# Masked attention scores: mask, scale and row maximum in one custom VectorE instruction a head, and the sums of v's weight quarters moved into the second group's round

## The chip, the cores and the metric

One core of one Trainium2 chip runs the whole program. The engines of the core are TensorE (PE, the matrix engine, with its weight load shown as PEld), VectorE (DVE), ScalarE (ACT), GpSimd (POOL) and SyncE (SP), which here issues every transfer between HBM and SBUF. The metric is the device time of one execution in microseconds (us). The kernel before took 2445.91 us, the median of five runs that lie between 2444.66 and 2451.15 us.

## What is computed

Two layers over 128 graphs (`x`, 128 x 128 nodes x 512 features, fp32) with one 128 x 128 adjacency matrix `adj` for all. The first layer multiplies scores with the adjacency and divides by the row's norm; the second is attention with 8 heads of 64, where missing edges are masked out. After each layer stand a residual sum and a layer norm.

```python
def layer0(x):
    q, k, v = x @ Wq0.T, x @ Wk0.T, x @ Wv0.T
    rel = adj.T * (q @ k.T)
    rel = rel / norm(rel, axis=2)
    return layernorm(x + rel @ v)

def layer1(x):
    q, k, v = (split into 8 heads) x @ Wq1 + bq1, x @ Wk1 + bk1, x @ Wv1 + bv1
    scores = q @ k.T / sqrt(64)
    scores = scores + where(adj == 0, -1e9, 0)
    return layernorm(x + softmax(scores) @ v)
```

The change concerns the line with the mask: for each head and each row the kernel needs the masked, scaled scores and the negated row maximum (`nmax`), which the exponential takes as its bias.

## The kernel before

**Groups and rounds.** Four graphs make a group, so there are NG = 32 groups; `g` counts groups and `b` the graphs within one. The program is a pipeline over rounds r = -1, 0, ..., 31. Round r holds the projections of layer 0 for group r + 1 (kinds `m`, which is Wq0 and Wk0 multiplied into one matrix, and `v0`) and those of layer 1 for group r (`q`, `k`, `v1`). Softmax and output of group r's attention run into the following round.

**Projections.** Each projection is a fast matrix product: seven products of half-size blocks, and one of these seven split once more into seven of quarter size. `Projection.step` emits them. Products 1, 6, 7 and 4 accumulate in one PSUM bank (`pa`), and between them VectorE reads intermediate sums out: L454 after product 6, L464 after product 7. Product 5 has a bank of its own (`pb`). The quarter products (L399, `inner`) run in two banks `pc2` and `pc3`; VectorE adds their results to the output at L405 and L425, and the next quarter product writes the same part of the bank, so it waits for those adds. The weights' own sums for the quarters are made once, by `inner_weight_sums` (L151 to L154, eight additions of 128 x 128 for each kind), and are read by the L399 products as `wd_...`. In the first group (`plain`) nothing is split a second time; products 2 and 3 use banks `pd` and `pe`, with the adds L451 and L459.

**Order of the work.** Nothing is scheduled automatically: `with tc.manual_schedule()` emits instructions in the order of a hand-made calendar. `dense` holds the steps of the projections; `short` holds everything else, entered with `at(r, k, function, ...)` at slot 35 r + k. The tables ZERO, STEADY, QUICK, LAST and INNER give the slots: STEADY for groups 0 to 29, QUICK for group 30, LAST for group 31, and INNER the slots of the quarter products. Each engine works off its instructions in that order, and all transfers are in SP's queue in that order.

**Attention of a group.** `attn_scores` lets PE make the scores of 8 heads into two PSUM banks (`ps`, four heads each, L542), arranged as four stretches of 32 columns with the heads between them. Then VectorE writes `w` = scores x 1/8 + mask in one instruction a bank (L551, SCALAR_TENSOR_TENSOR of 128 x 512). `attn_max`, a calendar entry of its own, takes the negated row maxima of four heads at once (L561, TENSOR_REDUCE). `attn_exp` makes the exponential and row sum of one head in each ScalarE instruction (L568). `attn_spill` and `attn_stage` take `w` out to HBM and back in another arrangement (`wd`, `wl`), `attn_transpose` (L587) turns 32 x 32 blocks, and `attn_out` multiplies with v (L600) and turns the result (L603). In STEADY graphs 0 and 1 stand at slot 32 and graphs 2 and 3 at slot 49, so that two graphs' scores come together.

**The last group.** `last_scores` does the same in one instruction a bank (L667) and one maximum over 8 heads (L670), `last_exp` is at L677, and the weights are turned by PE (`pwT`, L684, copied out at L686) instead of through HBM.

**Masks.** `masks` makes `maskp` (128 x 128: 0 or -1e9, L125) and then copies it four times, interleaved, into `mask` (128 x 512, L127), so that L551 can read it for four heads at once. It is entered at slot 8 of round -1, and the sums of v's quarters (`inner_weight_sums` of `v0` on VectorE) at slot 9 of round -1, both ahead of the first group's `m` adds.

Of the kernel before, what the change touches and what calls it, by code (L numbers as in the profile page):

```python
# [14 lines left out]
NEG = -1e9  # L15
# [3 lines left out]
def kernel(  # L19
# [98 lines left out]
    mhalf = const.tile([P, G], F32, name="mhalf")  # L118
    nc.vector.memset(mhalf, -0.5)

    maskp = const.tile([P, N], F32, name="maskp")
    mask = const.tile([P, D], F32, name="mask")

    def masks():
        nc.vector.tensor_scalar(maskp, adj_sb, 0.0, NEG, op0=ALU.is_equal, op1=ALU.mult)  # L125
        for a in range(H // 2):
            nc.vector.tensor_copy(mask.rearrange("p (q a r) -> p q a r", q=A, a=H // 2)[:, :, a, :],  # L127
                                  maskp.rearrange("p (q r) -> p q r", q=A))

# [404 lines left out]
    def attn_scores(g, b):  # L536

        p = [ps_m.tile([P, A, H // 2, Q], F32, tag="m", name=f"ps_{g}_{b}_{s}") for s in range(2)]
        for a in range(H // 2):
            for s in range(2):  # L540
                r = slice(s * HD, (s + 1) * HD)
                nc.tensor.matmul(p[s][:, :, a, :], QT[g][r, a, b, :], KT[g][r, a, b, :], start=True, stop=True)  # L542

        if g == NG - 2 and b >= 2:
            w = two.tile([P, 2, A, H // 2, Q], F32, tag="xl", name=f"w_{g}_{b}")
        else:
            if b % 2 == 0:
                WP[g, b // 2] = one.tile([P, 2, 2, A, H // 2, Q], F32, tag="yT" if b else "v0", name=f"w_{g}_{b}")
            w = WP[g, b // 2][:, b % 2]
        for s in range(2):  # L550
            nc.vector.scalar_tensor_tensor(w[:, s].rearrange("p q a r -> p (q a r)"),  # L551
                                           p[s].rearrange("p q a r -> p (q a r)"), HD ** -0.5, mask,
                                           op0=ALU.mult, op1=ALU.add)
        nmax = small.tile([P, H], F32, tag="nmax", name=f"nmax_{g}_{b}")
        sums = small.tile([P, H], F32, tag="sums", name=f"sums_{g}_{b}")
        SOFT[g, b] = [w, nmax, sums]

    def attn_max(g, b):
        w, nmax, _ = SOFT[g, b]
        for s in range(2):  # L560
            nc.vector.tensor_reduce(nmax[:, s * (H // 2):(s + 1) * (H // 2)], w[:, s].rearrange("p q a r -> p a q r"),  # L561
                                    axis=AX.XY, op=ALU.max, negate=True)

    def attn_exp(g, b, i0):
        w, nmax, sums = SOFT[g, b]
        for i in (i0, i0 + 1):
            s, a = divmod(i, H // 2)
            nc.scalar.activation(w[:, s, :, a, :], w[:, s, :, a, :], AF.Exp, bias=nmax[:, i:i + 1],  # L568
                                 accum_out=sums[:, i:i + 1])

    def attn_spill(g, b, s):
# [85 lines left out]
    def last_scores(g, b):  # L657
        p = [ps_m.tile([P, H // 2, P], F32, tag="m", name=f"ps_{g}_{b}_{s}") for s in range(2)]
        for a in range(H // 2):
            for s in range(2):  # L660
                r = slice(s * HD, (s + 1) * HD)
                nc.tensor.matmul(p[s][:, a, :], QT[g][r, a, b, :], KT[g][r, a, b, :], start=True, stop=True)
        if b == 0:
            LT["w"] = one.tile([P, 2, H, P], F32, tag="qT", name=f"w_{g}")
        w = LT["w"][:, b] if b < 2 else two.tile([P, H, P], F32, tag="xl", name=f"w_{g}_{b}")
        for s in range(2):
            nc.vector.scalar_tensor_tensor(w[:, s * (H // 2):(s + 1) * (H // 2)], p[s], HD ** -0.5,  # L667
                                           maskp[:, None, :].to_broadcast([P, H // 2, P]), op0=ALU.mult, op1=ALU.add)
        nmax = small.tile([P, H], F32, tag="nmax", name=f"nmax_{g}_{b}")
        nc.vector.tensor_reduce(nmax, w, axis=AX.X, op=ALU.max, negate=True)  # L670
        sums = small.tile([P, H], F32, tag="sums", name=f"sums_{g}_{b}")
        SOFT[g, b] = w, nmax, sums, graph(g, b)

    def last_exp(g, b, s):
        w, nmax, sums, _ = SOFT[g, b]
        for i in range(s * (H // 2), (s + 1) * (H // 2)):
            nc.scalar.activation(w[:, i, :], w[:, i, :], AF.Exp, bias=nmax[:, i:i + 1], accum_out=sums[:, i:i + 1])  # L677

    def last_transpose(g, b, s):
        if b % 2 == 0 and s == 0:  # L680
# [45 lines left out]
    def last_store(g, b):  # L726
# [14 lines left out]
        ((10.5, 11.5, 10.5, 11.5), 13.5, (18, 19, 21, 22), 23, (24, 25), (25, 26), (26, 28), (31, 32, 33, 34)),  # L741
    )
    STEADY = (
        (32, (32.5, 34.5, 35, 35, 35), (35, 37), 41.5, (44, 49, 51.5, 56, 60, 64.5, 68, 68)),
        (32, (35.5, 38.5, 38.5, 41.5, 41.5), (41.5, 41.5), 42, (47.5, 49, 51, 52, 61.5, 65, 69, 69)),
        (49, (49.5, 49.5, 52.5, 52.5, 52.5), (55, 55), 57.5, (58, 67, 67, 70, 73, 75, 77, 77)),
        (49, (50.5, 55, 55, 55, 55), (56.5, 58), 60.5, (64.5, 67, 69, 74.5, 76, 82, 83, 85.5)),
    )
    QUICK = (
        (31.5, (32, 33.5, 34.5, 34.5, 35), (35, 38), 40.5, (41, 43.5, 43.5, 47.5, 48.5, 50.5, 50.5, 52.5)),  # L750
        (36, (37, 37, 37, 37, 37), (39.5, 40.5), 41.5, (44.5, 45.5, 47.5, 50, 52, 53, 55, 62)),
        (37, (37.5, 41, 41, 41, 41), (41, 41), 45.5, (47.5, 50, 57.5, 57.5, 57.5, 59, 59.5, 64)),
        (37, (39, 41.5, 42.5, 44, 47), (44, 47), 49.5, (51, 52, 57.5, 61, 61, 64.5, 68.5, 68.5)),
    )
    LAST = (
        (17, (17, 17.5), (22, 22), (24, 24.5), 29, 35, 37.5),
        (17.5, (18, 19.5), (24, 25), (28.5, 33.5), 40.5, 48.5, 48.5),
        (19.5, (20, 23.5), (28.5, 29), (31, 37), 41.5, 51, 51.5),
        (23, (26.5, 26.5), (30.5, 31), (33.5, 41.5), 51, 51, 52.5),
    )  # L760


    INNER = (
        (2.71, 3.72, 8.23, 9.24, 3.26, 7.27, 8.28, 9.29),
        (5.71, 8.72, 9.23, 9.74, 5.26, 7.27, 8.28, 8.79),
        (2.71, 3.22, 6.73, 8.74, 2.76, 5.27, 7.28, 8.79),
    )

    RES = 59
# [17 lines left out]
    for g in range(NG):  # L787

        for h in range(2):
            if g:  # L790
                at(g - 2, 12, load_staged, g, h)
                at(g - 1, 12 + 4 * h, load, g, h)
        last = g == NG - 1

        sc, no, ou, de, ln, sp, st, tr = ZERO[0 if g == 0 else 2 if last else 1]
        for h in range(2):
            at(g - 1, sp[h], x1_spill, g, h)
            at(g - 1, st[h], x1_stage, g, h)
        for i, (dh, h) in enumerate(halves):
            at(g - 2, ((25.5, 27, 28.5, 30) if g != 1 else (22, 23, 24, 25))[i], x_transpose, g, dh, h)  # L800
            at(g - 1, tr[i], x1_transpose, g, dh, h)
        for b in range(G):
            at(g - 1, sc[b], l0_score, g, b)
            at(g - 1, ou[b], l0_out, g, b)
            at(g - 1, ln[b // 2], l0_layernorm, g, b)
        at(g - 1, no, l0_norm, g)
        at(g - 1, de, l0_rstd, g)

        if last:
            at(g, 2, last_residual, g)  # L810
        for b in range(G):
            if last:
                sc, e, t, o, st, no, w = LAST[b]
                at(g, sc, last_scores, g, b)
                for i in range(2):
                    at(g, e[i], last_exp, g, b, i)
                    at(g, t[i], last_transpose, g, b, i)
                    at(g, o[i], last_out, g, b, i)
                at(g, st, last_stats, g, b)
                at(g, no, last_norm, g, b)  # L820
                at(g, w, last_store, g, b)
                continue
            s, ex, sp, st, pk = QUICK[b] if g == NG - 2 else STEADY[b]
            at(g, s, attn_scores, g, b)
            at(g, ex[0], attn_max, g, b)
            for i in range(4):
                at(g, ex[i + 1], attn_exp, g, b, 2 * i)
            for i in range(2):
                at(g, sp[i], attn_spill, g, b, i)
            at(g, st, attn_stage, g, b)  # L830
            pieces = attn_transpose, attn_out, attn_back, attn_rows, attn_sum, attn_stats, attn_norm, attn_write
            for k, f in zip(pk, pieces):
                at(g, k, f, g, b)
                if f is attn_rows:
                    at(g, RES if g < NG - 2 and b < 2 else k, attn_res, g, b)

    at(-1, 8, masks)
    at(-1, 41, layer1_weights, "k", "k")
    for k, name, eng in ((9, "v0", nc.vector), (17, "m", nc.vector), (28, "q", nc.gpsimd), (49.5, "k", nc.gpsimd),
                         (52, "v1", nc.gpsimd)):  # L840
        at(-1, k, inner_weight_sums, name, eng)

# [41 lines left out]
```

## Time and profile before

The profiled execution took 2445.74 us; its span, from the first to the last recorded instruction, is 2444.0 us.

| quantity | value |
|---|---|
| median of five runs | 2445.91 us |
| profiled execution, its span | 2445.74 us, 2444.0 us |
| busy: PE, DVE, ACT, POOL | 99%, 81%, 41%, 47% of the span |
| one steady round | 74.66 us |
| L551, 248 instructions | 153.2 us busy, 680 ns each |
| L561, 248 instructions | 157.3 us busy, 676 ns each |
| L568 exponentials, 992 | 384.0 us busy, 395 ns each |
| L405 on 128 x 128 from PSUM | 281 to 291 ns each |
| L127 mask copies, 4 | 3.5 us busy, 940 ns each |

"Busy" counts an instruction from its start to its end. Consecutive instructions of one engine overlap by some 0.1 us, so the distance between two starts, the step, is shorter than the length. A list of waits names the engine that waits, the tile and line of the waiting instruction, what ended the wait, and then the total in us, the number of waits and the longest. In a timeline the first column is the start and the second the length in us; neighbouring instructions of one kind are merged into one row (x4), whose length runs from the first start to the last end; in brackets stands how long the engine had been idle, and what ended that.

### The profile page before, as it was taken

How to read it: one execution, taken by the hardware profiler on the slowest of the kernel's cores; microseconds unless marked ns; L12 is line 12 of the kernel's file. 1: busy time of each engine (PE TensorE's matmuls, PEld its weight loads, DVE VectorE, ACT ScalarE, POOL GpSimd, SP SyncE). 2: the span in 40 equal slices, each digit the busy share in tenths (PEclk: the TensorE clock that was granted, in tenths of full speed). 3: DMA queues.
4: the chain of work that ended last, by engine and by line, in shares of the span. 5: the costliest groups of instructions: out<-in, count | busy, mean ns of one | idle time of the engine just before them, and what ended most of it. 6: DMA issues, size and time to landing. Idle time of an engine off the chain costs nothing.

```text
span 2444.0 us, 48441 instructions
## 1 busy us (share of the span) xinstructions
PE 2419.0 (99%) x16552; PEld 2130.7 (87%) x16552; DVE 1976.6 (81%) x4409; ACT 1011.9 (41%) x3211; POOL 1138.6 (47%) x1796
## 2 busy tenths in 40 slices
PE   8999999999999999999999999999999999999997
PEld 5888888888888888888888888888888888888886
DVE  6678888788888788887888887888878888878888
ACT  1244344443443443444434434434444344344354
POOL 3625534445434355344454343553444543435544
PEclk9999999999999999999999999999999999999999
DMA  7356656566565666565665656665656656566564
GB/s 161 104 129 172 171 169 170 167 174 172 168 177 157 171 173 171 167 171 166 174 172 169 177 157 170 174 170 169 175 161 174 169 169 179 158 171 173 154 176 130
DMA packets 508600, 405.17 MB, mean 166 GB/s; under 512 B 37568, under 2 KB 424768, under 8 KB 508352
## 3 DMA queue, kind: packets, MB, share of 16 engines
q1 hardware_dynamic: 508352, 402.08, 59.6%
q8 instruction: 129, 2.11, 0.4%
q14 instruction: 119, 0.97, 0.1%
HBM read 237.31 MB, written 164.63 MB: 164 GB/s over the span
## 4 chain that ended last, share of the span: by engine, by line
PE 96%; DVE 2%; DMA 1%; issue 0%; POOL 0%; SPq 0%; POOLq 0%; ACT 0%; DVEq 0%
PE pa_v L358 18%; PE pa_q L358 9%; PE pa_k L358 9%; PE pa_m L358 9%; PE pc_v L399 8%; PE ps L542 5%; PE po L600 5%; PE pst L477 5%; PE pb_v L358 5%; PE po L522 4%; PE pc_k L399 4%; PE pc_q L399 4%; PE pc_m L399 4%; PE pb_q L358 2%; PE pb_k L358 2%; PE pb_m L358 2%
## 5 line engine op out<-in xcount | busy, mean ns | idle before, releaser
L568 ACT ACTIVATE w<-w,nmax 128x128 f32<-128x128 f32 x992 | 384.0, 395 | 116.2 <-DVE nmax L561 116.1
L502 POOL TENSOR_SCALAR ve<-st 128x1 f32<-128x1 f32 (+1 forms) x160 | 45.9, 287 | 745.4 <-DVE st L498 735.3
L358 PE MATMUL pa_v<-wc_v,tx 128*128 128x256 f32 x1536 | 363.7, 380 | 0.0
L358 PEld LDWEIGHTS pa_v<-wc_v,tx 128*128 128x128 f32 x1536 | 277.4, 190 | 30.3
L517 ACT ACTIVATE xr<-xr,sh,rstd 128x512 f32<-128x512 f32 x58 | 47.2, 815 | 411.4 <-POOL sh L512 411.4
L568 ACT ACTIVATION_READ_ACCUMULATOR w<-w,nmax 128x1 f32 x992 | 191.8, 193 | 0.0
L358 PE MATMUL pa_m<-tx,wc_m 128*128 128x256 f32 x768 | 184.0, 382 | 3.1 <-DVE yT L454 2.0
L405 DVE TENSOR_TENSOR v<-pc_v,v 128x256 f32<-128x256 f32 (+1 forms) x444 | 135.2, 310 | 58.3 <-PE pc_v L399 46.5
L358 PEld LDWEIGHTS pa_q<-tx,wc_q 128*128 128x128 f32 x768 | 143.2, 190 | 44.4 <-issue 29.3
L358 PE MATMUL pa_k<-tx,wc_k 128*128 128x256 f32 x768 | 181.8, 380 | 0.0
L358 PE MATMUL pa_q<-tx,wc_q 128*128 128x256 f32 x768 | 181.6, 379 | 0.2 <-DVE qT L454 0.2
L551 DVE SCALAR_TENSOR_TENSOR w<-ps,mask 128x512 f32<-128x512 f32 x248 | 153.2, 680 | 7.3 <-PE ps L542 7.3
L561 DVE TENSOR_REDUCE nmax<-w 128x4 f32<-128x512 f32 x248 | 157.3, 676 | 0.0
L358 PEld LDWEIGHTS pa_m<-tx,wc_m 128*128 128x128 f32 x768 | 138.5, 190 | 19.1 <-DVE yT L454 2.4
L587 DVE STREAM_TRANSPOSE wT<-wl 128x1024 f32<-128x1024 f32 x124 | 154.1, 1242 | 0.3 <-DMA xl_x<-in_x_dram 0.3
L358 PEld LDWEIGHTS pa_k<-tx,wc_k 128*128 128x128 f32 x768 | 138.4, 190 | 14.9
L631 POOL TENSOR_TENSOR xr<-xr,bv_b 128x512 f32<-128x512 f32 x58 | 73.7, 1270 | 139.2 <-DMA xr<-x1d 53.4
L369 ACT ACTIVATE qT<-pa_q,bq_sb 128x256 f32<-128x256 f32 x128 | 53.6, 470 | 205.0 <-PE pa_q L358 200.3
L399 PE MATMUL pc_v<-wd_v,ux 128*128 128x128 f32 x756 | 135.8, 275 | 0.2 <-DVE v L405 0.2
L405 DVE TENSOR_TENSOR qT<-pc_q,qT 128x128 f32<-128x128 f32 (+1 forms) x320 | 96.5, 309 | 44.4 <-PE pc_q L399 36.7
L522 PE MATMUL po<-v,rel 128*128 128x512 f32 x256 | 130.5, 593 | 0.0
L542 PE MATMUL ps<-kT,qT 64*128 64x128 f32 x1984 | 129.5, 279 | 0.0
(228 smaller groups left out, 6172.5 us busy)
## 6 DMA issues: line engine op xcount, KB each, us to landing
wd<-w SPq DMA_DIRECT2D x248, 256.0 KB, 3.0
wl<-wd SPq DMA_DIRECT2D x496, 128.0 KB, 3.0
xl_x<-in_x_dram SPq DMA_DIRECT2D x256, 128.0 KB, 6.0
x<-in_x_dram SPq DMA_DIRECT2D x64, 512.0 KB, 4.5
x1d<-x SPq DMA_DIRECT2D x64, 512.0 KB, 3.1
xl_h<-x1d SPq DMA_DIRECT2D x256, 128.0 KB, 2.9
od<-oT SPq DMA_DIRECT2D x496, 64.0 KB, 2.1
o<-od SPq DMA_DIRECT2D x118, 256.0 KB, 2.9
```

The costliest lines, as they stand in the source:

```text
L358: nc.tensor.matmul(bank[:, m, :], l[:, k, m * P:(m + 1) * P], r[:, k, :], start=start and m == 0 and k == 0, stop=(m == 1 and k == 1), ski ...
L399: nc.tensor.matmul(self.c[o][:, slot, :], l, r, start=start, stop=True, skip_group_check=True)
L405: nc.vector.tensor_tensor(y, self.c[o][:, slot], s if kept else y, op=ALU.add)
L477: nc.tensor.matmul(p, XT[g][:, dc, b, :], YT[g][:, dc, b, :], start=(dc == 0), stop=(dc == C - 1))
L522: nc.tensor.matmul(p, REL[g][0][:, b, :], V0[g][:, b, :], start=True, stop=True)
L542: nc.tensor.matmul(p[s][:, :, a, :], QT[g][r, a, b, :], KT[g][r, a, b, :], start=True, stop=True)
L551: nc.vector.scalar_tensor_tensor(w[:, s].rearrange("p q a r -> p (q a r)"), p[s].rearrange("p q a r -> p (q a r)"), HD ** -0.5, mask, op0= ...
L561: nc.vector.tensor_reduce(nmax[:, s * (H // 2):(s + 1) * (H // 2)], w[:, s].rearrange("p q a r -> p a q r"), axis=AX.XY, op=ALU.max, negat ...
L568: nc.scalar.activation(w[:, s, :, a, :], w[:, s, :, a, :], AF.Exp, bias=nmax[:, i:i + 1], accum_out=sums[:, i:i + 1])
L587: nc.vector.transpose(wT, SOFT[g, b][0].rearrange("p a i r -> p i a r"))
L600: nc.tensor.matmul(p[s * HD:(s + 1) * HD, a, :], V1[g][:, b, h * HD:(h + 1) * HD], wT[:, s * (H // 2) + a].rearrange("p q t -> p (q t)"), ...
L631: nc.gpsimd.tensor_tensor(xr, xr, bv_b, op=ALU.add)
```

## The change

Instead of `maskp` and `mask` there is one `mask` of 128 x 128 with 0 or -8e9. A new function `masked` makes one instruction for one head: out = (scores + mask) x (-1/8), and the minimum of `out` over the row goes into one column of `nmax`. That minimum of the negated values is the negated maximum. `attn_scores` and `last_scores` call it eight times a graph; `attn_max` and its calendar entries are gone; the exponentials read the negated `w` and so get `scale=-1.0`. In the built program each call is two VectorE instructions, one over 128 x 128 elements and one that writes the accumulated minimum to 128 x 1. The sums of v's quarters move from slot 9 to slot 38.5 of round -1, which is slot 3.5 of round 0. A number of calendar slots change. The order of PE's matmuls stays the same up to the last two groups, where a few pieces change places; in the rounds VectorE's order differs by the masked scores and by the place of two of the four `wl` transposes among their neighbours; GpSimd's order is unchanged.

```diff
-    maskp = const.tile([P, N], F32, name="maskp")
-    mask = const.tile([P, D], F32, name="mask")
+    mask = const.tile([P, N], F32, name="mask")

     def masks():
-        nc.vector.tensor_scalar(maskp, adj_sb, 0.0, NEG, op0=ALU.is_equal, op1=ALU.mult)
-        for a in range(H // 2):
-            nc.vector.tensor_copy(mask.rearrange("p (q a r) -> p q a r", q=A, a=H // 2)[:, :, a, :],
-                                  maskp.rearrange("p (q r) -> p q r", q=A))
+        nc.vector.tensor_scalar(mask, adj_sb, 0.0, NEG * HD ** 0.5, op0=ALU.is_equal, op1=ALU.mult)
+
+    def masked(dst, scores, m, least):
+        nc.vector.tensor_tensor_reduce(out=dst, in0=scores, in1=m, scale=-HD ** -0.5, scalar=3.0e38,
+                                       op0=ALU.add, op1=ALU.min, accum_out=least)
...
-        for s in range(2):
-            nc.vector.scalar_tensor_tensor(w[:, s].rearrange("p q a r -> p (q a r)"),
-                                           p[s].rearrange("p q a r -> p (q a r)"), HD ** -0.5, mask,
-                                           op0=ALU.mult, op1=ALU.add)
         nmax = small.tile([P, H], F32, tag="nmax", name=f"nmax_{g}_{b}")
+        for i in range(H):
+            s, a = divmod(i, H // 2)
+            masked(w[:, s, :, a, :], p[s][:, :, a, :], mask.rearrange("p (q r) -> p q r", q=A), nmax[:, i:i + 1])
...
-    def attn_max(g, b):
-        w, nmax, _ = SOFT[g, b]
-        for s in range(2):
-            nc.vector.tensor_reduce(nmax[:, s * (H // 2):(s + 1) * (H // 2)], w[:, s].rearrange("p q a r -> p a q r"),
-                                    axis=AX.XY, op=ALU.max, negate=True)
...
-            nc.scalar.activation(w[:, s, :, a, :], w[:, s, :, a, :], AF.Exp, bias=nmax[:, i:i + 1],
+            nc.scalar.activation(w[:, s, :, a, :], w[:, s, :, a, :], AF.Exp, bias=nmax[:, i:i + 1], scale=-1.0,
                                  accum_out=sums[:, i:i + 1])
...
-        for s in range(2):
-            nc.vector.scalar_tensor_tensor(w[:, s * (H // 2):(s + 1) * (H // 2)], p[s], HD ** -0.5,
-                                           maskp[:, None, :].to_broadcast([P, H // 2, P]), op0=ALU.mult, op1=ALU.add)
         nmax = small.tile([P, H], F32, tag="nmax", name=f"nmax_{g}_{b}")
-        nc.vector.tensor_reduce(nmax, w, axis=AX.X, op=ALU.max, negate=True)
+        for i in range(H):
+            s, a = divmod(i, H // 2)
+            masked(w[:, i], p[s][:, a], mask, nmax[:, i:i + 1])
...
     STEADY = (
-        (32, (32.5, 34.5, 35, 35, 35), (35, 37), 41.5, (44, 49, 51.5, 56, 60, 64.5, 68, 68)),
-        (32, (35.5, 38.5, 38.5, 41.5, 41.5), (41.5, 41.5), 42, (47.5, 49, 51, 52, 61.5, 65, 69, 69)),
-        (49, (49.5, 49.5, 52.5, 52.5, 52.5), (55, 55), 57.5, (58, 67, 67, 70, 73, 75, 77, 77)),
-        (49, (50.5, 55, 55, 55, 55), (56.5, 58), 60.5, (64.5, 67, 69, 74.5, 76, 82, 83, 85.5)),
+        (32, (32.5, 34.5, 35, 35, 35), (35, 36.5), 41.5, (44, 49, 51.5, 56, 60, 64.5, 68, 68)),
+        (32, (35.5, 38.5, 38.5, 41.5, 41.5), (41.5, 41.5), 42, (47.5, 49, 51, 52, 60, 65, 69, 69)),
+        (49, (49.5, 49.5, 50.5, 50.5, 52.5), (55, 55), 57.5, (58.5, 67, 67, 70, 73, 75, 77, 77)),
+        (49, (50.5, 55, 55, 55, 55), (56.5, 56.5), 60.5, (63.5, 67, 69, 74.5, 76, 82, 83, 85.5)),
     )
...
     LAST = (
-        (17, (17, 17.5), (22, 22), (24, 24.5), 29, 35, 37.5),
-        (17.5, (18, 19.5), (24, 25), (28.5, 33.5), 40.5, 48.5, 48.5),
-        (19.5, (20, 23.5), (28.5, 29), (31, 37), 41.5, 51, 51.5),
-        (23, (26.5, 26.5), (30.5, 31), (33.5, 41.5), 51, 51, 52.5),
+        (17, (17, 17.5), (20, 22), (24, 24.5), 29, 35, 37.5),
+        (17.5, (17.5, 19.5), (24, 24.5), (28, 31), 40, 45.5, 46),
+        (19.5, (20, 23.5), (28.5, 29), (31, 37), 41, 51, 51),
+        (23, (23.5, 27), (29.5, 32), (33.5, 41.5), 51, 53, 54.5),
     )
...
     INNER = (
         (2.71, 3.72, 8.23, 9.24, 3.26, 7.27, 8.28, 9.29),
-        (5.71, 8.72, 9.23, 9.74, 5.26, 7.27, 8.28, 8.79),
-        (2.71, 3.22, 6.73, 8.74, 2.76, 5.27, 7.28, 8.79),
+        (5.71, 8.72, 9.23, 9.74, 4.26, 7.27, 8.28, 8.79),
+        (2.71, 3.22, 6.73, 8.24, 2.76, 4.77, 6.78, 8.79),
     )
...
-            at(g, ex[0], attn_max, g, b)
...
-    for k, name, eng in ((9, "v0", nc.vector), (17, "m", nc.vector), (28, "q", nc.gpsimd), (49.5, "k", nc.gpsimd),
+    for k, name, eng in ((38.5, "v0", nc.vector), (17, "m", nc.vector), (28, "q", nc.gpsimd), (49.5, "k", nc.gpsimd),
                          (52, "v1", nc.gpsimd)):
```

## The prediction

> **What bounds the kernel now.** I read the page's first part, then TensorE's (PE's) waits, then the timelines of PE and VectorE (DVE) at the start, in one steady round and at the end.
>
> ```profile
> PE 2419.0 (99%) x16552; PEld 2130.7 (87%) x16552; DVE 1976.6 (81%) x4409; ACT 1011.9 (41%) x3211; POOL 1138.6 (47%) x1796
> ```
>
> ```profile
> PE pa_m L358 <- DVE yT L454: 2.0, 1, 2.0
> ```
>
> PE is busy 99% of the span and its named waits come to some 15 us, each met once or twice. A steady round (from one `po` L600 at 1199.25 to the next at 1273.91 us: 74.66 us) has no PE wait at all. So work taken off DVE in the rounds is worth nothing. The change can win only at the start and the end, and can lose wherever DVE now answers PE late.
>
> **The change, part by part.**
>
> *1. The start.* Four mask copies go, and the eight sums of v's quarters leave.
>
> ```profile
> 33.99 3.52 DVE L127 COPY mask<-maskp 128x128 f32<-128x128 f32 x4
> ...
> 43.95 0.68 DVE L454 TENSOR_TENSOR yT<-pa_m,yT 128x512 f32<-128x512 f32 x1
> ```
>
> ```profile
> 40.77 1.89 PE L358 MATMUL pe_m<-xT,wc_m 128*128 128x256 f32 x8
> 44.69 1.99 PE L358 MATMUL pa_m<-tx,wc_m 128*128 128x256 f32 x8 [2.04 <-DVE yT L454]
> ```
>
> The columns are start, length, engine, line. The add L454 stands behind copies (3.52) and sums (L151 to L154, twice, 37.43 to 43.95: 6.5 us). Its own input, the product at 37.31, ends at 39.20. In the changed order only the one mask instruction (0.94 at 33.01) stands ahead, so L454 starts at 39.2 and PE goes on at 40.77 + 1.73 = 42.50 instead of 44.69: 2.19 us, and the 0.10 by which the first matmul after a wait is longer (1.99 against 1.89 for eight). I take -2.3. The later waits there (L464, ACT yT, POOL sq) are chains of their own and move along; the DMA share is 0.00 in 50 to 60 us, so no load is late for the next group.
>
> The sums come back in the next round, behind the first two adds of `pc_m`, at 67.85 on before's clock. Eight equal sums (wd_m, 47.40 to 49.59) took 2.2 us. Cover: PE needs the pair of adds behind them at 72.95, and 67.85 + 2.2 + 0.6 = 70.65. Without it (GpSimd busy beside them, as in 37.43 to 43.95) they take 6.5, the pair ends at 74.95, and 2.0 us of the gain is given back. I take 0: GpSimd runs mostly short instructions there until 70.13.
>
> *2. The masked scores in the rounds.* For each sequence two L551 and two L561 become eight instructions, and in the built program each is two: the 128-element pass and a read of its accumulator into one column of `nmax`. Step from start to start decides, not length.
>
> ```profile
> 1202.41 2.49 DVE L551 SCALAR_TENSOR_TENSOR w<-ps,mask 128x512 f32<-128x512 f32 x4 [0.22 <-PE ps L542]
> ...
> 1205.67 0.62 DVE L405 TENSOR_TENSOR v<-pc_v,v 128x128 f32<-128x128 f32 x2 [0.77 <-PE pc_v L399]
> 1206.20 1.27 DVE L561 TENSOR_REDUCE nmax<-w 128x4 f32<-128x512 f32 x2
> ```
>
> ```profile
> 1207.20 0.61 PE L399 MATMUL pc_v<-wd_v,ux 128*128 128x128 f32 x4
> ```
>
> An L551 steps by (2.49 - 0.68)/3 = 0.60, an L561 by 0.60, so a sequence costs DVE 2.4 us. The new pass reads 128 elements from PSUM and a mask from SBUF, as L405 does, which steps by 0.21 where nothing holds it:
>
> ```profile
> 1245.72 0.29 DVE L405 TENSOR_TENSOR v<-pc_v,v 128x128 f32<-128x128 f32 x1
> 1245.93 0.41 DVE L405 TENSOR_TENSOR v<-pc_v,s_v 128x256 f32<-128x256 f32 x1
> ```
>
> The accumulator read on DVE is in no row. Bounds:
>
> ```profile
> 0.80 0.09 DVE L117 MEMSET ones<- 128x32 f32 x1 [0.80 <-PEq L870]
> 0.83 0.06 DVE L119 MEMSET mhalf<- 128x4 f32 x1
> ...
> 1258.79 0.18 DVE L498 BATCH_NORM_AGGREGATE st<-bs 128x2 f32<-128x6 f32 x1
> 1258.88 0.73 DVE L629 TENSOR_TENSOR o<-o,rs 128x512 f32<-128x512 f32 x1
> ```
>
> ```profile
> 1207.28 0.19 ACT L568 ACTIVATION_READ_ACCUMULATOR w<-w,nmax 128x1 f32 x1
> 1207.37 0.39 ACT L568 ACTIVATE w<-w,nmax 128x128 f32<-128x128 f32 x1
> ```
>
> Below: a memset, which like the read has no input in memory, steps by 0.03. Above: DVE's aggregate and ScalarE's own accumulator read step by 0.09; farther out, the latter's whole length, 0.19. A head then costs p = 0.24, 0.30 or 0.40 us. I take 0.05 for the read, nearer to the memset as the row of the same engine without an input, so p = 0.26 and 8p = 2.1 us a sequence. DVE's total hardly moves; what moves is the place. Scores, mask and maximum now stand in one block, where the maxima used to stand behind the adds.
>
> The tightest place is two sequences at once. The block starts at 1202.41 and takes 16p instead of 2.4. Behind it stand the two L405 (0.61 for the pair, the second waits for the first), and in the built program the third of the four matmuls at 1207.20, at 1207.42, waits for the second L405; PE starts 0.05 after such an end (44.64 to 44.69). So 1202.41 + 16p + 0.66 <= 1207.42, p <= 0.272. At 0.26 there is 0.2 us to spare and the cost is 0. Above, each of 30 rounds loses 16(p - 0.272) + 0.11, and nothing takes it up, since PE has no other wait. The other block (1241.72, before the matmuls at 1247.38) allows 1241.72 + 16p + 0.74 + 0.05 <= 1247.38, p <= 0.304.
>
> PSUM: the first bank is freed after 4p instead of one L551; the next user, `pb_q` at 1205.47, waits for the fourth head, 1202.41 + 4p = 1203.5. ScalarE's exponentials get their first maximum some 4 us sooner and nothing else on its queue changes length. The transfers are the same in number; half-spills stand somewhat earlier on SP's queue, behind exponentials that are also earlier. The moved transposes of `wl` feed products with no PE wait now.
>
> *3. The last but one group.* Block of one sequence at 2368.56; L425 behind it is awaited by PE at 2370.58. 2368.56 + 2.08 + 0.29 + 0.05 = 2370.98: 0.40 + 0.11 lost. The following 16 heads start at about 2372.7 (scores, shifted by that), end at 2376.9, and the next L425 ends at 2377.2 against PE's 2375.71 + 0.5: 1.0 + 0.1 lost. The wait at 2379.57 (0.19 and 0.11) goes, as a maximum no longer stands there. Sum +1.3.
>
> *4. The last group.* DVE is the chain from 2405.8 on.
>
> ```profile
> 2406.52 1.29 DVE L667 SCALAR_TENSOR_TENSOR w<-ps,maskp 128x512 f32<-128x512 f32 x2
> 2407.84 1.22 DVE L670 TENSOR_REDUCE nmax<-w 128x8 f32<-128x1024 f32 x1
> 2408.98 0.68 DVE L454 TENSOR_TENSOR v<-pa_v,v 128x512 f32<-128x512 f32 x1
> ```
>
> 2.46 us a sequence become 2.08: four times 0.38, -1.5. The reordered transposes and products I take at 0, bounds -2 and +1 (a copy of 0.6 now stands ahead of L464, which PE awaits).
>
> **Sum:** -2.3 - 1.5 + 1.3 = -2.5 us on a span of 2444.0; the profiled execution took 2445.74 (1.74 around its span), 0.17 under the median of 2445.91. So 2443.4.
>
> **Rivals.**
>
> *A. DVE answers late in every round (slower).* With p = 0.30 the place at 1207.42 loses 16 x 0.028 + 0.11 = 0.56, 30 times: +16.8, or 2460 with the rest. For it: the steps of 0.09 in two rows, and that no other PE wait absorbs it. Against: the memset row. It passes 0.2% (4.9 us, about what a measurement here can tell from no change) once 30(16(p - 0.272) + 0.11) > 7.4, from p = 0.280. Chance 0.33, 0.04 of it still within 0.2%.
>
> [...]
>
> *B. The read costs ScalarE's full 0.19.* p = 0.40: 30 x (2.05 + 0.11) and, at 1247.38, 30 x (1.54 + 0.11), together +114: 2560. DVE's aggregate is as long (0.18) and steps by 0.09, so 0.08.
>
> *C. Faster.* p = 0.24 gives the last group 4 x 0.54 = 2.2 and the last but one only +0.7; the first exponential, which waits 4.77 us for `nmax` at 2409.09, comes up to 2 us sooner and with it transposes and products: -2.3 - 2.2 + 0.7 - 1.7 = -5.5, 2440.4. Against: DVE, not ScalarE, is the chain there. 0.17.
>
> *D. The sums meet GpSimd:* 2.0 of the gain is lost, 2445.4; it lies inside the forecast's own case.
>
> **How the numbers follow.** Forecast (no stall in the rounds, within 0.2%) 0.42, A 0.33, B 0.08, C 0.17. Faster 0.17, same 0.42 + 0.04 = 0.46, slower 0.29 + 0.08 = 0.37. The range goes from a little below C, 2439.5, to A at p = 0.30, 2461; about 0.18 is left out, nearly all above. The forecast's own range is 2441 to 2446.
>
> **What would show it.** The step between two heads' passes is p: below 0.272 PE has no wait on DVE at `pc_v` L399 in the rounds; above it, one wait a round on `v` L405, of 16(p - 0.272). The wait of `pa_m` on L454 at the start is gone and the eight wd_v sums take about 2.2 us. A round that is still 74.66 us long bears the forecast out; one of 75.2 is rival A.

## The result and the profile after

The changed kernel took 2442.16 us (median of 25 executions, 2441.09 to 2444.67). The kernel before took 2447.74 us (median of 43, 2444.66 to 2451.86; the first five of these gave the 2445.91 that the prediction was made against). The ratio is 0.9978, 95% interval [0.9973, 0.9984]: 0.22% faster, hardly over what a measurement here can tell from no change. The profiled execution of the changed kernel took 2444.12 us, its span is 2442.3 us.

The page's first part, busy time of each engine, and four of PE's waits in the changed kernel:

```profile
PE 2420.9 (99%) x16552; PEld 2131.6 (87%) x16552; DVE 1866.4 (76%) x5945; ACT 1005.4 (41%) x3211; POOL 1139.5 (47%) x1796
```

```profile
PE pc_v L399 <- DVE v L425: 1.3, 1, 1.3
...
PE po L695 <- DVE wT L680: 0.9, 1, 0.9
...
PE pa_m L358 <- DVE yT L464: 0.9, 1, 0.9
PE pc_m L399 <- DVE yT L405: 0.6, 1, 0.6
```

VectorE's busy time fell by 110 us, PE's rose by 1.9, and the time moved by no more than 0.2%. All waits of PE are again met once. The wait of 2.0 us on L454 is gone; one of 0.6 on L405, at 73.04, is new (before had one of 0.3 at 66.56).

Three stretches, cut at instructions that every version has, show where time goes. *Start*: from the first product of v (`pa_v`, 21.70 us before) to the product behind the first group of quarter products (`pa_m`, 73.39). *Rounds*: from there to the last group's first scores (2405.32). *End*: from there to the end of the span.

| trace | start | rounds | end | half clock seen in the start |
|---|---|---|---|---|
| before | 51.69 | 2331.93 | 38.68 | no |
| changed | 51.69 | 2332.02 | 36.92 | yes |
| changed, heads longer (below) | 49.53 | 2331.62 | 36.94 | no |

(In the other traces the rounds take 2331.8 to 2332.0.) So the rounds are worth nothing, the end gave 1.76 us, and the start gave 2.16 us in one execution and nothing in another. PE's timeline in the start of the changed kernel:

```profile
42.46 1.89 PE L358 MATMUL pa_m<-tx,wc_m 128*128 128x256 f32 x8
...
53.67 2.96 PE L358 MATMUL pa_m<-xT,wc_m 128*128 128x256 f32 x8 [1.11 <-DVE xT L212]
56.42 2.65 PE L522 MATMUL po<-v,rel 128*128 128x512 f32 x4
...
73.04 0.49 PE L399 MATMUL pc_m<-ux,wd_m 128*128 128x128 f32 x2 [0.59 <-DVE yT L405]
73.36 1.89 PE L358 MATMUL pa_m<-tx,wc_m 128*128 128x256 f32 x8
```

The product at 42.46 stood at 44.69 before: 2.23 us gained. Then two groups of matmuls take 2.96 and 2.65 us that took 1.99 and 1.88 in the kernel before: 1.74 us lost. The two rows before:

```profile
56.00 1.99 PE L358 MATMUL pa_m<-xT,wc_m 128*128 128x256 f32 x8 [1.11 <-DVE xT L212]
57.83 1.88 PE L522 MATMUL po<-v,rel 128*128 128x512 f32 x4
```

The table of one-microsecond stretches says why; after the stretch and its length come PE, PEld, DVE, ACT and POOL busy, and then the granted TensorE clock:

```profile
51.00:52.00 1.00, 0.27 (x3) 0.08 (x1) 0.29 (x1) 0.00 (x0) 0.51 (x2) 1.00 0.00 0
52.00:53.00 1.00, 0.42 (x8) 0.16 (x8) 0.38 (x2) 0.00 (x0) 0.08 (x1) 1.00 0.00 0
53.00:54.00 1.00, 0.33 (x2) 0.31 (x3) 1.00 (x2) 0.00 (x0) 0.98 (x1) 1.00 0.00 0
54.00:55.00 1.00, 1.00 (x5) 0.86 (x4) 0.96 (x3) 0.00 (x0) 0.05 (x1) 0.78 0.02 8
55.00:56.00 1.00, 1.00 (x4) 0.72 (x4) 1.00 (x2) 0.00 (x0) 0.33 (x1) 0.50 0.00 0
56.00:57.00 1.00, 1.00 (x3) 0.66 (x2) 0.97 (x2) 0.29 (x1) 0.92 (x3) 0.50 0.00 0
57.00:58.00 1.00, 1.00 (x2) 0.33 (x1) 0.20 (x1) 0.30 (x1) 1.00 (x3) 0.52 0.00 0
```

PE was busy for only 1.0 of the 3 us from 51 to 54 (it waits for the norm's chain through DVE and GpSimd), and then ran at half clock for (0.22 + 0.50 + 0.50 + 0.48) / 0.5 = 3.4 us. Its longest idle time in this place was 1.11 us. The kernel before has the same idle place at 53.5 to 56.0 (PE busy for 1.03 of the 3 us from 53 to 56) and kept full clock in its profile: 1.00 in every microsecond from 50 to 61. Why half clock follows the place in one execution and not in another, no run here shows.

The rest of the gain went to the sums of v, which met GpSimd. (Two of the seven half-size products, 2 and 3, are split into quarters and not one, as the section on the kernel before has it; hence eight sums, four for each.) VectorE's and GpSimd's timelines there:

```profile
67.84 0.29 DVE L154 TENSOR_TENSOR wc_v<-wc_v,wd_v 128x128 f32<-128x128 f32 x1
68.05 0.70 DVE L151 TENSOR_TENSOR wd_v<-wc_v 128x128 f32<-128x128 f32 x1
...
70.01 1.33 DVE L154 TENSOR_TENSOR wc_v<-wc_v,wd_v 128x128 f32<-128x128 f32 x1
71.26 0.60 DVE L405 TENSOR_TENSOR yT<-pc_m,yT 128x128 f32<-128x128 f32 x2
```

```profile
67.92 0.68 POOL L201 COPY wc_k<-wk_s 128x512 f32<-128x512 f32 x1
...
69.91 1.27 POOL L157 TENSOR_TENSOR wc_k<-wk_s,wc_k 128x512 f32<-128x512 f32 x1
```

From the moment GpSimd copies the `k` weights, a sum takes 0.6 to 1.3 us instead of 0.28. Each of the four slow sums ends 0.14 to 0.16 us behind the GpSimd instruction that was running when it started (70.01 + 1.33 = 71.34 against 69.91 + 1.27 = 71.18), as though it waited for that one. The eight take 4.3 us (66.99 to 71.26), the pair of adds behind them is late, and PE waits 0.59 us at 73.04.

The heads, in the round that the prediction worked with:

```profile
1202.04 0.29 DVE L127 CUSTOM_DVE_ANT_0 w<-ps,mask 128x128 f32<-128x128 f32 x1 [0.27 <-PE ps L542]
1202.26 0.08 DVE L127 DVE_READ_ACCUMULATOR2_ANT nmax<- 128x1 f32 x1
1202.26 0.28 DVE L127 CUSTOM_DVE_ANT_0 w<-ps,mask 128x128 f32<-128x128 f32 x1
...
1205.42 0.08 DVE L127 DVE_READ_ACCUMULATOR2_ANT nmax<- 128x1 f32 x1
1205.42 0.61 DVE L405 TENSOR_TENSOR v<-pc_v,v 128x128 f32<-128x128 f32 x2
```

```profile
1206.79 0.61 PE L399 MATMUL pc_v<-wd_v,ux 128*128 128x128 f32 x4
```

Sixteen heads take 3.38 us, so a head steps by p = 0.211 us. The accumulator read is 0.08 us long and adds nothing: the next pass starts in the same instant. The pair of adds ends at 1206.03, a microsecond before PE's third matmul (1207.01) needs it.

### The profile page after: what moved, and what is told of

It is laid out like the page before. It is cut to its first block, busy times and chain, and to the rows that moved or that the text cites. A ratio compares the mean times of both kernels' runs of the same rounds, so it can differ in the third digit from the quotient of the medians.

```text
span 2442.3 us, 49798 instructions
## 1 busy us (share of the span) xinstructions
PE 2420.9 (99%) x16552; PEld 2131.6 (87%) x16552; DVE 1866.4 (76%) x5945; ACT 1005.4 (41%) x3211; POOL 1139.5 (47%) x1796
## 4 chain that ended last, share of the span: by engine, by line
PE 96%; DVE 2%; issue 1%; DMA 1%; POOL 0%; ACT 0%; SPq 0%; POOLq 0%; DVEq 0%
PE pa_v L358 18%; PE pa_m L358 9%; PE pa_q L358 9%; PE pa_k L358 9%; PE pc_v L399 8%; PE ps L542 5%; PE po L594 5%; PE pst L477 5%; PE pb_v L358 4%; PE po L522 4%; PE pc_k L399 4%; PE pc_q L399 4%; PE pc_m L399 4%; PE pb_m L358 2%; PE pb_q L358 2%; PE pb_k L358 2%
## 5 line engine op out<-in xcount | busy, mean ns | idle before, releaser
L502 POOL TENSOR_SCALAR ve<-st 128x1 f32<-128x1 f32 (+1 forms) x160 | 56.5, 353 | 745.1 <-DVE st L498 735.7
L127 DVE CUSTOM_DVE_ANT_0 w<-ps,mask 128x128 f32<-128x128 f32 x1024 | 221.7, 286 | 16.6 <-PE ps L542 15.8
L562 ACT ACTIVATION_READ_ACCUMULATOR w<-w,nmax 128x1 f32 x992 | 198.8, 200 | 0.0
L405 DVE TENSOR_TENSOR v<-pc_v,v 128x256 f32<-128x256 f32 (+1 forms) x444 | 135.2, 309 | 69.9 <-PE pc_v L399 58.0
L405 DVE TENSOR_TENSOR qT<-pc_q,qT 128x128 f32<-128x128 f32 (+1 forms) x320 | 98.4, 315 | 54.1 <-PE pc_q L399 46.4
L366 ACT COPY yT<-pa_m 128x512 f32<-128x512 f32 x64 | 37.5, 585 | 243.4 <-DVE v L405 115.9
L627 POOL TENSOR_TENSOR xr<-xr,o 128x512 f32<-128x512 f32 x58 | 74.0, 1275 | 124.8 <-issue 122.5
```

What stands on the lines that cost most here:

```text
L127: nc.vector.tensor_tensor_reduce(out=dst, in0=scores, in1=m, scale=-HD ** -0.5, scalar=3.0e38, op0=ALU.add, op1=ALU.min, accum_out=least)
L405: nc.vector.tensor_tensor(y, self.c[o][:, slot], s if kept else y, op=ALU.add)
L627: nc.gpsimd.tensor_tensor(xr_, xr_, o.rearrange("p (f a r) -> p f a r", f=A, a=H // 2), op=ALU.add)
```

## The experiments

Theory: (1) VectorE's place in the rounds is free up to p = 0.269 and costs PE from there (the prediction's condition on the rows above: 1202.04 + 16p + 0.66 <= 1207.01); (2) the end is won by the fused instruction, the start by the shorter masks; (3) what the start wins is sometimes taken back by half clock, which in the changed kernel's profile came behind the idle place of PE (54.6 to 58.0 us), and by GpSimd. The main rivals are named in each expectation. Times are medians of the executions; "before" is the kernel before on the same chip in the same session.

**Both kernels again** (no edit).

> The kernel before, once more, for the clock and span of each execution. Theory T (half clock): the executions of before above 2449 us differ from those near 2445.5 by 3.4 us windows at half TensorE clock around the stalls of the start (42 to 56 us); each such window costs PE about 1.7 us, so an execution 4 to 5 us above the fastest should show a mean granted clock lower by some 0.002 to 0.004. Rival (loads): the clock is the same, 0.999, in all, and the time goes to transfers. Median expected 2446 to 2449.

Measured: 2447.19 us (11 executions, 2445.99 to 2451.99), before beside it 2448.39 (33), ratio 0.9999 [0.9990, 1.0008]. Over all executions of the kernel before in this study that list a clock (102): mean granted clock 0.999, 16 executions, median 2446.15 us; 0.998, 27, 2447.07; 0.997, 28, 2448.89; 0.996 or less, 31, 2451.22. Time and clock go together, as the theory said, and the rival of the transfers, with the same clock in all, falls. An execution 5 us longer shows 0.003 less clock, that is 0.003 x 2448 = 7 us of full clock; a part of it may lie behind waits, and the clock is listed only to 0.001, which is 2.4 us. Where in the kernel the clock is lost, these means do not say.

> The changed kernel, once more, to get a profile without the half clock at 54.5 to 58.0 us that its first profile shows. Theory T: median 2442.1; an execution near 2441.8 has full clock until 2430 us, its PE stands 2.2 us ahead of before from 42.5 until about 70, and keeps 1.2 to 2.0 of it behind 75 us; the end (2405 on) gives 1.7 to 2.0. Rival (the gain of the start is given back in any case by the sums of v, which meet GpSimd): PE is level with before at 75 us although no clock was lost, and the whole gain comes from the end.

Measured: 2442.71 us (11, 2441.08 to 2447.07), ratio 0.9981 [0.9972, 0.9990]. Its profile (2445.14 us) caught half clock in another place, at 24.8 to 28.2 us, behind a wait of 3.33 us for the first `x` at the very start; its start stretch is 51.09, end 36.98. That half clock cost it 1.7 us (two groups of matmuls need 2.34 and 2.87 us from start to start instead of 1.80 and 1.73), so its start would be 49.4 without. A trace without half clock anywhere in the start came from a later kernel whose start is the same (heads_longer, below), with 49.53. In both the gain is kept: the rival that it is lost in any case falls.

**The sums left where they were.**

```diff
-    for k, name, eng in ((38.5, "v0", nc.vector), ...
+    for k, name, eng in ((9, "v0", nc.vector), ...
```

> The change with the sums of v's quarters left at slot 9 of round -1. By the rows: sums start at 34.0 behind the one mask instruction, take 6.5 us beside GpSimd and end at 40.5; L454 starts there, 1.2 us later than in the changed kernel, ends at 41.2, and PE needs it only at 42.46, so PE waits for nothing there. If so the moved sums bring nothing: same time as the changed kernel or 0.3 to 0.6 us faster, 2441.6, as no sums meet GpSimd at 68 us and the wait of 0.59 us at 73.04 is gone. Rival (the sums had to move): a wait of pa_m on yT L454 of 1 us or more comes back, time 2443 or more.

Measured: 2442.52 us (11, 2441.33 to 2446.07), ratio 0.9977 [0.9968, 0.9985]; no wait on L454. Its VectorE and PE rows:

```profile
39.67 1.24 DVE L154 TENSOR_TENSOR wc_v<-wc_v,wd_v 128x128 f32<-128x128 f32 x1
40.84 0.68 DVE L454 TENSOR_TENSOR yT<-pa_m,yT 128x512 f32<-128x512 f32 x1
```

The sums take 7.3 us beside GpSimd, so L454 starts late (its input was there at 38.8), and still PE has the result before it needs it at 42.06. Both this trace and the changed kernel's first one have the half clock in the start; the start stretch is 50.82 here and 51.69 there. The moved sums thus cost 0.87 us in such an execution and bring nothing; between the medians (2442.52 and 2442.71) there is no difference, where 0.3 to 0.6 was thought possible: what made L454 late before was the sums *and* the copies, and taking away the copies is enough.

**Only the sums moved**, in the kernel before.

```diff
-    for k, name, eng in ((9, "v0", nc.vector), ...
+    for k, name, eng in ((38.5, "v0", nc.vector), ...
```

> The kernel before, with nothing but the sums of v's quarters moved to slot 38.5 of round -1. The four mask copies end at 37.5, before L454's input at 39.2, so the wait of 2.0 us at 44.69 goes here too. Theory: same start as the changed kernel, and the end of the kernel before: slower than the changed kernel by what the end gave, 1.7 to 2.0 us, so median 2443.9 and lowest 2443. If the masks and not the sums made L454 late, the wait stays and the time is before's.

Measured: 2445.89 us (11, 2443.84 to 2449.40), ratio 0.9990 [0.9981, 0.9999]. The wait on L454 is gone, the start is 52.11 with half clock, the end 38.68 as before. So either half of the edit at the start mends it. The median is 2 us over the expected 2443.9. The lowest times put the end's share at 2443.84 - 2441.08 = 2.8 us, the traces at 1.76; the 1 us between is not explained.

**A longer head**, twice.

```diff
+    fill = const.tile([P, 96], F32, name="fill")
...
             masked(w[:, s, :, a, :], p[s][:, :, a, :], ..., nmax[:, i:i + 1])
+            if g < NG - 2:
+                nc.vector.memset(fill, 0.0)
```

> The changed kernel with one more VectorE instruction behind every head in groups 0 to 29, a memset of 128 x 96 to a tile that nobody reads. It makes the step p of a head longer; the prediction's formula says what a longer p costs. A memset is expected to add 0.05 to 0.12, so p = 0.26 to 0.33. Theory (the place at 1207.42 decides, PE needs the second L405): below p = 0.269 nothing; above it each of 30 rounds loses 16 (p - 0.269) + 0.11, and above 0.304 the second block loses as well. p = 0.31 gives 30 x 0.77 + 30 x 0.2 = 29 us at most, 2465 to 2471; p = 0.29 gives 13 us, 2455. Rival (a later head costs nothing, since the adds could stand later or PE has other slack): 2442 whatever p is.

Measured: 2443.79 us (7, 2441.46 to 2444.33), ratio 0.9974 [0.9964, 0.9985], no wait of PE in the rounds. VectorE's timeline:

```profile
1200.64 0.23 DVE L128 CUSTOM_DVE_ANT_0 w<-ps,mask 128x128 f32<-128x128 f32 x1
1200.79 0.08 DVE L128 DVE_READ_ACCUMULATOR2_ANT nmax<- 128x1 f32 x1
1200.85 0.14 DVE L557 MEMSET fill<- 128x96 f32 x1
1200.90 0.23 DVE L128 CUSTOM_DVE_ANT_0 w<-ps,mask 128x128 f32<-128x128 f32 x1
```

A head now steps by 0.26, which is the p of the prediction, and it is free, as the prediction said: the trace's rounds take 2331.62 us. The median doesn't show it, being 1.1 to 1.6 us over the changed kernel's: five of the seven executions lie near 2444, where the changed kernel has 8 of 25, and so few can't tell the two apart. This profile also is the changed kernel's start without half clock (the memsets begin later). PE there:

```profile
22.11 1.97 PE L359 MATMUL pa_v<-wc_v,xT 128*128 128x256 f32 x8 [1.68 <-DVE xT L213]
...
54.21 1.99 PE L359 MATMUL pa_m<-xT,wc_m 128*128 128x256 f32 x8 [1.11 <-DVE xT L213]
56.05 1.88 PE L523 MATMUL po<-v,rel 128*128 128x512 f32 x4
...
71.64 1.89 PE L359 MATMUL pa_m<-tx,wc_m 128*128 128x256 f32 x8
```

The start is 71.64 - 22.11 = 49.53 against 51.69: 2.16 us kept. The eight sums took 66.12 to 68.49, 2.4 us: at full clock they are through when GpSimd's copies begin (68.57; in the second trace of the changed kernel 71.31 and 71.39).

The second time the memset has 128 x 144 (`fill` of [P, 144]).

> As heads_longer, where 128 x 96 made the step of a head 0.260 us and cost nothing (no wait of PE in the rounds), but the memset is 128 x 144, so p should be about 0.31. Theory (first block: p up to 0.269; second block: up to 0.304): each of 30 rounds loses 16 (0.31 - 0.269) + 0.11 = 0.77 and 16 (0.31 - 0.304) + 0.11 = 0.2 us, 29 us in all: 2471, with waits of pc_v or pc_q L399 on adds of VectorE in every round. If p comes out as 0.29: 13 us, 2455. Rival (PE has slack behind the block that the formula misses): under 2446.

Measured: 2471.53 us (4, 2469.82 to 2473.55), ratio 1.0091 [1.0077, 1.0105]; p = 0.310. PE's waits, and the wait in its timeline:

```profile
PE pc_v L400 <- DVE v L406: 15.2, 30, 0.5
```

```profile
1221.74 0.49 PE L400 MATMUL pc_v<-wd_v,ux 128*128 128x128 f32 x2 [0.51 <-DVE v L406]
```

Laid against the trace with p = 0.26, PE falls behind in each round by 0.77 us at the first block and by 0.20 at the second; 0.77 and 0.2 were expected. The rival that PE has slack there falls.

**The old instructions in the last group**, in the new calendar.

```diff
-        for i in range(H):
-            s, a = divmod(i, H // 2)
-            masked(w[:, i], p[s][:, a], mask, nmax[:, i:i + 1])
+        for s in range(2):
+            nc.vector.scalar_tensor_tensor(w[:, s * (H // 2):(s + 1) * (H // 2)], p[s], HD ** -0.5,
+                                           mask[:, None, :].to_broadcast([P, H // 2, P]), op0=ALU.mult, op1=ALU.add)
+        nc.vector.tensor_reduce(nmax, w, axis=AX.X, op=ALU.max, negate=True)
```

(The exponentials of that group lose their `scale=-1.0` again.)

> The changed kernel, but the last group's scores with the two old instructions a bank and one maximum over 8 heads (2.46 us a sequence instead of 8 x 0.211 = 1.69), in the new calendar. Theory (VectorE is the chain from 2410 on, two to four sequences of 0.77 us lie on it): 1.5 to 3.1 us slower than the changed kernel, median 2444.2 to 2445.5. Rival (the end is gained by the calendar alone): same as the changed kernel.

Measured: 2446.25 us (11, 2443.66 to 2450.58), ratio 0.9990 [0.9981, 0.9999]. PE's timeline in the end, of the kernel before, of this kernel and of the changed one:

```profile
2417.25 0.71 PE L399 MATMUL pc_v<-wc_v,ux 128*128 128x128 f32 x4 [1.88 <-DVE v L425]
```

```profile
2417.20 0.71 PE L399 MATMUL pc_v<-wc_v,ux 128*128 128x128 f32 x4 [2.92 <-DVE v L425]
```

```profile
2416.27 0.71 PE L399 MATMUL pc_v<-wc_v,ux 128*128 128x128 f32 x4 [1.34 <-DVE v L425]
```

The end is 38.82 us long, against 36.92 and 38.68 (before): the instruction is worth 1.9 us, the calendar's changes nothing (0.1 to the bad). The median lies farther off, 3.5 to 4 us, than the trace, and above the expected 2444.2 to 2445.5; whether the longer idle place of PE (2.92 us) has to do with that was not shown.

**The old instructions in groups 0 to 29**, maxima as entries of their own.

```diff
+            at(g, (32.5, 35.5, 49.5, 50.5)[b], attn_max, g, b)
```

(with L551 and `attn_max` of the kernel before, `scale=1.0` in their exponentials, and the wide mask)

> The changed kernel, but groups 0 to 29 with the old instructions and the maxima as an entry of their own at the old slots (the wide mask is copied by ScalarE in round 0). Theory (work taken off VectorE in the rounds is worth nothing): the same time as the changed kernel, median 2442.2 to 2443, round of 74.66 us, no wait of PE in the rounds. Rival (the rounds gained by the fused instruction): slower by some 30 x 0.05 = 1.5 us or more.

Measured: 2443.65 us (11, 2442.69 to 2447.91), ratio 0.9979 [0.9971, 0.9988]. That is some 1 to 1.5 us over the changed kernel, more than expected, but not in the rounds: start 51.69, rounds 2331.95, the same to 0.1 us, and PE stays level to 2421 us. The end is 37.99, 1.05 too long, and the excess lies behind all arithmetic, in SyncE's wait for the last store:

```profile
SPq L892 <- DMA out_dram<-o: 2.8, 1, 2.8
```

In the other traces this wait is 1.7 us. In this trace alone a transfer of instructions (queue q14) falls into the last 3 us of the span. That it delays the store was not tested. For the question asked the rounds are decided: the 85 us of VectorE time that the fused instruction saves there (1951.6 busy here, 1866.4 in the changed kernel) are worth nothing.

**Matmuls in PE's idle places.** The identity is multiplied with itself into banks that are overwritten.

```diff
+        if g == 0:
+            for _ in range(7):
+                nc.tensor.matmul(pn, ident, ident.rearrange("p (g q) -> p g q", g=G), start=True, stop=True)
...
+                if self.name == "m_1":
+                    for _ in range(9):
+                        nc.tensor.matmul(self.a[:, 0, 0:P], ident, ident, start=True, stop=True)
```

> The changed kernel with the sums at slot 9, and matmuls of the identity on itself (7 ahead of the first pn, 9 ahead of the first product of m of group 1; their results are overwritten) in the two places where PE stands idle at 51 to 54 us. [...] Rival (the half clock has nothing to do with PE's idle time there): the same spread, 2441.3 to 2446, median 2442.5.

Measured: 2443.32 us (8, 2442.72 to 2443.89), ratio 0.9977 [0.9967, 0.9988]. No half clock in the start, and all executions within 1.2 us; but the matmuls took 1.73 and 2.27 us in gaps of 0.86 and 1.1, so the start is 50.74 and the median lies above the 2441.5 or less that was hoped for.

> As keep_warm, where 7 and 9 matmuls took 1.73 and 2.27 us in idle places of 0.86 and 1.1 us and so cost 1.3 us themselves, but kept the half clock away in all 8 executions (2442.7 to 2443.9). Now 3 and 4 of them, 0.74 and 0.98 us, which fit. Theory T: no half clock at 50 to 60 us, median 2441.3 to 2442, nearly all executions under 2443. Rival: they are too few, spread as in the changed kernel.

Measured: 2442.18 us (7, 2441.68 to 2445.47), ratio 0.9973 [0.9962, 0.9984]: five executions under 2442.6, two near 2445. The profile is of one of these two: full clock from 50 to 60 us, but half clock at 24 to 27 us, behind a wait of 3.0 us for the first `x`, which these matmuls do not cover. In the times nothing is shown: 2 of 7 executions lie above 2443, and 8 of 25 of the changed kernel. In the profiles the place tells more: half clock follows it in seven of the eleven without such matmuls, and in none of the three with them (before_warm, next, is the third).

> The kernel before with such matmuls in its idle places at the start: 8 behind the first pe_m (42.6 to 44.6 us, ahead of the product that waits for L454), 3 ahead of pn and 4 ahead of the first product of m of group 1. No wait and no stall is removed. Theory T (what spreads the executions of before from 2445 to 2452 is the half clock after idle windows at 42 to 56 us): executions at 2445 to 2446.5, median near 2445.8, that is 2 to 3 us below before of the same chip. Rival (the spread has another cause, or comes from the end): median as before, 2447.5 to 2448.5.

Measured: 2446.53 us (11, 2444.75 to 2448.10), before beside it 2449.29 (17, 2445.88 to 2452.32), ratio 0.9989 [0.9980, 0.9998]. So its median is 2.8 us lower (0.5 to 4.9 by the interval), and the median of the mean granted clocks is 0.998 against 0.997. This is what clock lost behind idle PE at the start would give back. It is less than the theory said: six of the 11 executions lie above 2446.5. Its profile shows one more such place, in the end; PE's timeline, and rows of one microsecond, in which the third number from the end is the granted clock:

```profile
2416.85 0.71 PE L399 MATMUL pc_v<-wc_v,ux 128*128 128x128 f32 x4 [1.88 <-DVE v L425]
...
2418.70 3.52 PE L358 MATMUL pa_v<-wc_v,tx 128*128 128x256 f32 x8
```

```profile
2419.00:2420.00 1.00, 1.00 (x3) 0.82 (x3) 1.00 (x3) 0.00 (x0) 1.00 (x1) 0.50 0.00 0
2420.00:2421.00 1.00, 1.00 (x4) 0.73 (x4) 0.97 (x2) 0.00 (x0) 0.19 (x1) 0.50 0.00 0
```

This lengthens its end from 38.68 to 39.57.

**A copy of the end on ScalarE**, with the sums at slot 9.

```diff
-        copy = nc.scalar.copy if b == G - 1 and s else nc.vector.tensor_copy
+        copy = nc.scalar.copy if (b, s) in ((0, 0), (G - 1, 1)) else nc.vector.tensor_copy
```

> The changed kernel with the sums at slot 9, and the first copy of turned weights in the last group (L680, graph 0, heads 0 to 3) made by ScalarE, which stands idle from 2416.5 to 2420 us, instead of VectorE, where it takes 0.6 us ahead of L464 and L425, for which PE waits 1.34 us. Theory (that copy lies on the chain of the end): the wait of pc_v on v L425 falls to 0.7 us, the end comes 0.4 to 0.6 us sooner, lowest time 2440.6 to 2440.9 against 2441.1 to 2441.3, median about 2441.7. Rival (the chain goes through ScalarE or the scores after it): same time as the changed kernel with the sums at slot 9, 2442.5, lowest 2441.3.

Measured: 2441.56 us (10, 2440.93 to 2445.59), ratio 0.9974 [0.9964, 0.9983].

```profile
2417.70 0.71 PE L399 MATMUL pc_v<-wc_v,ux 128*128 128x128 f32 x4 [0.74 <-DVE v L425]
```

The wait fell from 1.34 to 0.74 and the end from 36.92 to 36.39, as expected. Half of the executions are at 2440.93 to 2441.20, under nearly all of the changed kernel; between medians the 0.6 us can't be told from nothing. It is the version that I would keep.

## Why the prediction came out as it did

The forecast was 2443.4 us; 2442.16 was measured, inside the range (2439.5 to 2461) and inside the forecast's own (2441 to 2446). The gain of 0.22% is on the border between the cases "within 0.2%" and "faster". That the time came so near is in part luck: the forecast started from 2445.91, which over more executions became 2447.74, and so the gain between the medians is 5.6 us and not 2.5.

*Step 1, the start, -2.3:* right in size and mechanism. PE's product was put at 42.50 and came at 42.46; of the 2.23 us, 2.16 stand behind the first quarter products when the clock holds. What the step lacked is the clock: in the first profile 1.74 us went to half clock. The sums were put at 2.2 us without GpSimd (2.4 measured) and at 6.5 beside it, with 2.0 given back (rival D); beside it they took 4.3 and gave back 0.87. In the traces they met GpSimd's copies where half clock had come just before, and not in the two where it had not.

*Step 2, the rounds:* the condition p <= 0.272 is right to a few hundredths of a microsecond (p = 0.26 free, p = 0.31 costs 0.77 + 0.20 a round), and with it the weight of rival A. The term that was mis-sized is the accumulator read: 0.05 was taken for its step, between 0.03 and 0.19, and it is 0.00, so p = 0.211 and not 0.26, below the lower bound. An instruction whose length lies wholly beside its neighbours was not thought of, though the prediction itself said that the step decides.

*Step 3, the last but one group, +1.3:* measured +0.1 (2331.93 to 2332.02). For the 16 heads the working was right and p was not: 2372.14 + 16 x 0.211 + 0.29 + 0.05 = 2375.86, and PE's matmul stands at 2375.86. At p = 0.26 it would have been 0.8 later. The 0.51 at the block of one sequence had a second fault: the block was put at 2368.56 and starts at 2368.03, so that even p = 0.26 would have lost nothing there (2368.03 + 2.08 + 0.34 = 2370.45, and PE's matmul stands at 2370.53).

*Step 4, the last group, -1.5:* measured -1.76. With p = 0.211 four sequences save 4 x (2.46 - 1.69) = 3.1, but until 2410 PE and not VectorE sets the pace in the changed kernel (VectorE waits there for `pa` and `ps`), so not all four lie on the chain. A larger saving a sequence and fewer sequences nearly cancel, so that -1.5 came close is luck. The reorders at 0 were right (0.1); the copy ahead of L464 that the step named costs 0.5 to 0.6 (end 36.92 to 36.39, wait 1.34 to 0.74).

*The sum:* -2.2 + 0.1 - 1.8 = -3.9 us without half clock, 2445.74 - 3.9 = 2441.8, where most executions of the changed kernel lie. Rival C (faster, 2440.4, by a shorter p) named the direction in which the forecast missed. A, B fell with p.

*What stays open:* the medians differ by 5.6 us, the lowest times by 2444.66 - 2441.09 = 3.6. The 2 us between are most likely lost clock that the kernel before meets more often: its mean granted clock is 0.997 in the median and the changed kernel's 0.998, which is some 2.4 us of full clock. It has one idle place of PE more (2.04 us at 42.6) and a longer one (1.88 instead of 1.34 at the end). Filling the idle places of its start took 2.8 us off its median, but which of them counts for how much was not separated. Nothing in the one profile of before could have shown it: it is of an execution with full clock.

## What to carry to other kernels

For work on an engine that is not the bound, write down by when the bound engine needs what is queued behind it: start of the block + number x step + the rest <= the need. That line forecast the cost of a longer head to 0.01 us a round, while 110 us less busy time were worth nothing. And a stall of the matrix engine cost twice in some executions here, once as a stall and once as half clock behind it (3.4 us of it in the changed kernel's profile, 1.74 us lost), so removing short stalls at the start and the end can be worth more in the median than in one profile.

## What the runs showed of the hardware

- DVE's read of its accumulator is 0.083 us long and costs no time between two passes (step 0.211 with it in the changed kernel, the same as L405's 0.21 without it in the kernel before). A memset behind it adds 0.05 us at 128 x 96 and 0.10 at 128 x 144 (the two kernels with longer heads).
- Half clock came in pieces of 3.4 us behind stretches in which PE did little: in the changed kernel's first profile behind 51 to 54 us, busy for 1.0 of the 3, in its second behind a wait of 3.33 us, and in before_warm's profile behind one idle time of 1.88 us at the end. The kernel before has the same 1.88 us and 1.03 busy us of 3 at its start, and kept full clock behind both in its profile. With matmuls without use at 51 to 54 us it did not come in three profiles; without them it came in seven of eleven.
- An addition of 128 x 128 in SBUF takes DVE 0.28 us, and mostly 0.6 to 1.4 us while GpSimd works on tiles of 128 x 512 (in the kernel before 0.28 at 47.40 to 49.59 us, and 0.70 to 1.35 in five of six begun at 37.43 to 42.27).
